# Two edge tiles per ScalarE sum in the first layer of a two-layer graph network: ranks packed into one number, split again on GpSimd, and a new written-out order

## The chip, the core and the metric

The kernel runs on one core of a Trainium2 chip. Time is device time in microseconds (us) of one execution. The engines are named as in the profile: PE (TensorE matmul) and PEld (its weight loads), DVE (VectorE), ACT (ScalarE), POOL (GpSimd) and SP (SyncE, which here only issues DMAs).

## The reference, cut to what matters

There are N = 12500 nodes with 256 features and E = 200000 edges `(src, dst, edge_weight)`, sorted by `dst`. The first layer computes, with `row = src` and `col = dst`:

```
feat_self, feat_nei = relu(x @ W[0] + b[0]), relu(x @ W[1] + b[1])     # 4 heads of 32
edge_w = (leaky(att_s)[row] + leaky(att_n)[col]) * adj_vals
agg    = segment_sum(edge_w * feat_nei[col], row)                      # sums over src
x      = layernorm(x + concat(norm(feat_self), norm(agg)))
```

The second layer sends `relu(x[src] @ W_a + x[dst] @ W_b + b)` to `dst`, sums it there, and ends in a linear update and two more normalisations. The change touches the first layer alone.

## The kernel before, in words

The edges come sorted by `dst`, while the first layer sums over `src`. So the first layer writes every edge's message into a log in DRAM, grouped by block of 128 source nodes (98 blocks and one for what is left over, `NBX` = 99; `NBE` = 100 is that made even). A second stage then reads the log block by block and sums. A third stage does the second layer.

**Groups.** The 1563 tiles of 128 edges are taken 14 at a time (`GT`), which makes 112 groups. `sort_tasks(g)` holds the tasks of a group as small functions, `feat_tasks(g)` those that compute node features, `meta_tasks` those that prepare edge data for eight groups at once. The tasks of one group, in the order of their data:

- `widen` (ACT, L564) copies the block numbers of the first 7 tiles into `bx`, each one 99 times. `hot` (DVE, L568) compares `bx` with a row of 0 to 98, which makes the one-hot rows `A` of those tiles. `hot_b` (DVE, L572) does the other 7 tiles straight from the block numbers, read with step 0. `pair` (DVE, L576) adds the halves into `B`.
- `ranks` (PE, L584), `quarter` (ACT, L587), `rows` (DVE, L591), `begins` (PE, L595 to L599) and `keep_begins`, `keep_v` (ACT, L603, L606) count the edges by block and give `v`: for each edge lane and block, the place where its run begins.
- `place_mm0` to `place_mm2` (PE, L622 and L624) write into a PSUM bank `wp`, for 5, 5 and 4 tiles, `v + BIG * A`, with `BIG` = 4096.
- `pick0` to `pick13` (ACT, L651) take one tile each: an ACTIVATE of `relu(w - BIG)` over 99 elements, whose sum (the one place of that edge) is written by a second instruction, the accumulator read, into a column of `sl`.
- `split` (DVE, L658 to L660), `hot_r`, `hot_q`, `goods` (DVE, L664, L674, L669: `rh`, `qh`, `mv`) and `permute` (PE, L681) turn places into a permutation by matmul; `mv` is the last DVE input of `permute`.
- `rel_keep` (ACT, L686: `rs`), `extras` (DVE, L697 copies the source row into the message tile `m`, L698 sums), `rel_turn`, `rel_row`, `rel_out`, `rel_in` (a row through DRAM and back, on SP's queue) and `hot_n` (DVE, L709: `oT`) make the one-hot matrices by target node.
- `message0` to `message5` (PE, L718) with `evict0` to `evict5` (ACT, L725) compute the messages into `m`, and `scatter0` to `scatter3` (POOL, L731) send `m` to the log by indirect DMAs.

**The order.** PE, ACT, DVE and SP run their instructions in the written order, and POOL runs its own in the order of the program. The dictionary `AT` gives each task a place; group `g`'s task is put at `256 * g + AT[name]`, and all tasks are issued in that order. So a group is spread over some seven periods of 256 steps, and within one period each engine works on tasks of several groups. An instruction whose input isn't ready holds everything behind it on its engine.

**Buffers.** PSUM has 8 banks: 2 for `wp`, 2 for the banks of the counts, 3 for `mp` (used by `permute` and the messages), 1 for `tp`.

Of the kernel before, what the change touches and what calls it, by code (L numbers as in the profile page):

```python
# [11 lines left out]
def _warn_once_fixed(msg, *args, **kwargs):  # L12
# [6 lines left out]
FT = mybir.dt.float32  # L19
FR = mybir.dt.float32r  # L20
BF = mybir.dt.bfloat16
I32 = mybir.dt.int32
AF = mybir.ActivationFunctionType
OP = mybir.AluOpType
AX = mybir.AxisListType

P = 128
# [3 lines left out]
GT = 14  # L31
NR = 16
RW = 4
MW = HD + H + 2
# [5 lines left out]
AT = {  # L40
    "widen": -453, "hot": -365, "hot_b": -265, "pair": -179, "ranks": -86, "quarter": -64, "rows": -29,
    "begins": 13, "keep_begins": 55, "keep_v": 51, "shift": 161, "reach": 262, "steps": 227, "steps_keep": 243,
    "steps_low": 256, "target": 313, "index": 400, "place_mm0": 52, "place_mm1": 63, "place_mm2": 204,
    "pick0": 73, "pick1": 78, "pick2": 78, "pick3": 87, "pick4": 123, "pick5": 144, "pick6": 156, "pick7": 170,
    "pick8": 179, "pick9": 219, "pick10": 229, "pick11": 239, "pick12": 249, "pick13": 280, "split": 339,
    "hot_r": 358, "goods": 374, "hot_q": 371, "permute": 424, "rel_keep": 435, "extras": 477, "rel_turn": 502,
    "rel_row": 552, "rel_out": 574, "rel_in": 595, "hot_n": 959, "message0": 997, "evict0": 1053,
    "message1": 1032, "evict1": 1063, "message2": 1056, "evict2": 1082, "message3": 1065, "evict3": 1121,
    "message4": 1101, "evict4": 1165, "message5": 1188, "evict5": 1203, "scatter0": 1120, "scatter1": 1146,
    "scatter2": 1197, "scatter3": 1206, "load": -331, "transposes": 47, "keep": 68, "project": 80, "relu": 295,  # L50
    "att_mult": 355, "mean_sum": 459, "att_sum": 438, "centre": 467, "leaky_n": 498, "part0": 584, "part1": 636,
    "part2": 665, "part3": 705, "leaky_s": 585, "out_f": 634, "m_load": -1689, "m_cast0": -1234,
    "m_cast1": -1433, "m_col0": -1201, "m_keep0": -1125, "m_col1": -698, "m_keep1": -614, "m_col2": -941,
    "m_keep2": -861, "m_block": -1073, "m_place": -877, "m_high": -378, "m_rest": -285, "m_mid": 263,
    "m_low": 351, "m_win": -76, "m_turn": -866, "m_pairs": -710, "m_mask": -535, "m_count": 210,
}
BIG = 4096.0
MAGIC = 1.5 * 2.0 ** 23
# [42 lines left out]
def kernel(  # L101
# [19 lines left out]
    nc = tc.nc  # L121
# [18 lines left out]
    NBX = NB + 1  # L140
    NBE = NBX + NBX % 2
# [74 lines left out]
    with ExitStack() as l0:  # L216
# [27 lines left out]
        nbig = dcp.tile([P, 1], FT, name="nbig")  # L244
        nc.vector.memset(nbig, -BIG)
        quart = dcp.tile([P, 1], FT, name="quart")
        capc = dcp.tile([P, 1], FT, name="capc")
# [59 lines left out]
        raw, blk, em, twin = {}, {}, {}, {}  # L307
# [240 lines left out]
        def sort_tasks(g):  # L548
# [4 lines left out]
            st = {}  # L553
            CH = [(0, 5), (5, 5), (10, 4)]

            def small(name, w=1, dt=FT, bufs=2, p=NBX):
                st[name] = srt.tile([p, w], dt, name=name, bufs=bufs)
                return st[name]
# [3 lines left out]
            def widen():  # L562
                st["bx"] = srt.tile([P, h, NBX], BF, name="bx")
                nc.scalar.copy(st["bx"], blk[c][:, j * GT:j * GT + h, None].to_broadcast([P, h, NBX]))  # L564

            def hot():
                st["A"] = srt.tile([P, GT, NBX], BF, name="A", bufs=3)
                nc.vector.tensor_tensor(st["A"][:, :h], iotab[:, :h], st["bx"], op=OP.is_equal)  # L568

            def hot_b():  # L570
                b = blk[c][:, j * GT + h:j * GT + GT, None].to_broadcast([P, h, NBX])
                nc.vector.tensor_tensor(st["A"][:, h:], iotab[:, h:], b, op=OP.is_equal)  # L572

# [31 lines left out]
            def keep_v():  # L605
                nc.scalar.copy(small("v", NBE, FR, p=P), st["V"])  # L606

# [9 lines left out]
            def place_mm(i):  # L617
                def f():
                    a, n = CH[i]
                    wp = st["w", i] = ps.tile([P, 512], FT, name="wp")  # L620
                    o = wp[:, :n * NBE].rearrange("p (t b) -> p t b", b=NBE)
                    nc.tensor.matmul(o, identr, st["v"][:, None, :].to_broadcast([P, n, NBE]),  # L622
                                     start=True, stop=False)
                    nc.tensor.matmul(o[:, :, :NBX], identk, st["A"][:, a:a + n],  # L624
                                     start=False, stop=True)
                return f
# [18 lines left out]

            def place_pick(t):
                def f():
                    i, k = divmod(t, 5)
                    if t == 0:
                        small("sl", GT, p=P)  # L650
                    nc.scalar.activation(small("junk", NBX, BF, p=P), st["w", i][:, k * NBE:k * NBE + NBX], AF.Relu,  # L651
                                         bias=nbig, accum_out=st["sl"][:, t:t + 1])
                return f

            def split():
# [39 lines left out]
            def extras():  # L695
                m = st["m"] = msgp.tile([P, NR, MW], FT, name="m")
                nc.vector.tensor_copy(m[:, :, MW - 2], st["go"][:, :, 1])  # L697
                nc.vector.tensor_reduce(m[:, :, MW - 1], st["go"][:, :, 2:5], AX.X, OP.add)  # L698

            def rel_out():  # L700
# [28 lines left out]
            def scatter(k):  # L729
                def f():  # L730
# [7 lines left out]
                    for p in zeros[-16:] if g >= GZ else zeros[:nz0] if g < 2 else []:  # L738
                        tc.add_manual_dep(ins, p.name, sync_dep, reason="the rows left over are zero")
                return f  # L740

            tasks = dict(widen=widen, hot=hot, hot_b=hot_b, pair=pair, ranks=ranks, quarter=quarter,
                         rows=rows, begins=begins, keep_begins=keep_begins, keep_v=keep_v, shift=shift, reach=reach,
                         steps=steps, steps_keep=steps_keep, steps_low=steps_low, target=target, index=index)
            tasks.update((f"place_mm{i}", place_mm(i)) for i in range(3))
            tasks.update((f"pick{t}", place_pick(t)) for t in range(GT))
            tasks.update(split=split, hot_r=hot_r, goods=goods, hot_q=hot_q, permute=permute, rel_keep=rel_keep,
                         extras=extras, rel_turn=rel_turn, rel_row=rel_row, rel_out=rel_out, rel_in=rel_in, hot_n=hot_n)
# [48 lines left out]

        work = defaultdict(list)
        for name, fs in (("hot_b", (first_nodes, lambda: load_group(1), load_norm_consts, bias_parts, bases)),
                         ("rows", (mt["m_high"], lead_zero, mt["m_rest"], mt["m_mid"], mt["m_win"])),  # L800
                         ("shift", (mt["m_turn"], mt["m_pairs"], mt["m_low"], consts_pairs)),
                         ("att_mult", (mt["m_mask"], mt["m_count"])),
                         ("centre", (consts_places, base_places))):
            work[min(AT[name], AT["split"] - 1) + 0.5] += fs

# [885 lines left out]
```

## Time and profile before

| | |
|---|---|
| five runs, median (lowest to highest) | 4010.7 us (4005.71 to 4014.55) |
| the profiled execution: time, span of its instructions | 4009.71 us, 4007.8 us |
| mean granted TensorE clock | 0.985 of full speed |
| first stage: first and last `hot_n` start | 50.7 us and 1059.5 us |
| second stage, the log's sums | about 1060 to 1990 us |
| third stage, the second layer | about 1990 us to the end |
| busy share of the whole span | PE 89%, PEld 74%, DVE 79%, ACT 59%, POOL 67% |

How to read it: busy shares are over the whole span; the stages have different limits, and the change lies in the first. In a timeline the columns are the start (us), the duration (us), the engine, the line, the operation and the tiles. ACT and DVE records overlap, since an instruction's start-up and drain run beside its neighbours. So what an instruction costs its engine is the time from its start to the next start, not its duration. A group row ends in busy time and the mean duration of one, then the idle time just before them.

### The profile page before, as it was taken

How to read it: one execution, taken by the hardware profiler on the slowest of the kernel's cores; microseconds unless marked ns; L12 is line 12 of the kernel's file. 1: busy time of each engine (PE TensorE's matmuls, PEld its weight loads, DVE VectorE, ACT ScalarE, POOL GpSimd, SP SyncE). 2: the span in 40 equal slices, each digit the busy share in tenths (PEclk: the TensorE clock that was granted, in tenths of full speed). 3: DMA queues.
4: the chain of work that ended last, by engine and by line, in shares of the span. 5: the costliest groups of instructions: out<-in, count | busy, mean ns of one | idle time of the engine just before them, and what ended most of it. 6: DMA issues, size and time to landing. Idle time of an engine off the chain costs nothing. (4 is left out here: it accounts for less than half of the span.)

```text
span 4007.8 us, 82564 instructions
## 1 busy us (share of the span) xinstructions
PE 3555.5 (89%) x24976; PEld 2971.5 (74%) x24976; DVE 3181.3 (79%) x9205; ACT 2377.1 (59%) x8379; POOL 2667.2 (67%) x2542
## 2 busy tenths in 40 slices
PE   8999999999899999999978888888888888888887
PEld 6888888887688888888866666666666666666665
DVE  8999999999799999999856666666666666666665
ACT  7999999999522222222255555555555555555555
POOL 2555555555666666666477777777777777777776
PEclk8999999999899999999999999999999999999999
DMA  5887866666666666666466666666666666666665
GB/s 176 277 275 272 275 219 220 218 216 200 219 185 193 184 195 192 187 192 194 145 182 171 170 172 170 170 169 171 173 169 171 171 171 170 170 172 172 170 171 135
DMA packets 470159, 763.55 MB, mean 191 GB/s; under 512 B 76202, under 2 KB 313504, under 8 KB 469712
## 3 DMA queue, kind: packets, MB, share of 16 engines
q1 hardware_dynamic: 339552, 415.13, 36.7%
q0 software_dynamic: 110848, 327.87, 27.2%
q10 hardware_dynamic: 19312, 15.21, 1.2%
q8 instruction: 204, 3.34, 0.3%
q14 instruction: 243, 1.99, 0.2%
HBM read 559.81 MB, written 198.12 MB: 189 GB/s over the span
## 5 line engine op out<-in xcount | busy, mean ns | idle before, releaser
L1346 POOL DMA_INDIRECT gb<-pd,srcf x1563 | 1508.4, 965 | 493.5 <-issue 237.1
L1405 DVE TENSOR_TENSOR gb<-qp,gb 128x512 f32<-128x512 f32 x781 | 538.7, 690 | 700.4 <-DMA gb<-pd,srcf 494.1
L1424 PE MATMUL agg<-gb,o 128*128 128x256 f32 x3126 | 857.5, 397 | 228.4 <-ACT gb L1407 224.3
L1407 ACT ACTIVATE gb<-gb 128x512 f32<-128x512 f32 x781 | 490.9, 629 | 846.9 <-DVE gb L1405 845.0
L731 POOL DMA_INDIRECT log<-m,ix x448 | 545.9, 1219 | 520.4 <-ACT m L725 149.5
L1424 PEld LDWEIGHTS agg<-gb,o 128*128 128x128 f32 x3126 | 562.3, 192 | 432.6 <-ACT gb L1407 371.3
L972 PE MATMUL sum<-lg,o 128*128 128x256 f32 x3724 | 838.4, 379 | 13.0 <-DMA lg<-log 12.0
L972 PEld LDWEIGHTS sum<-lg,o 128*128 128x128 f32 x3724 | 696.6, 189 | 112.0 <-POOL lg L959 12.2
L964 DVE TENSOR_SCALAR o<-iotap,lg 128x128 f32<-128x128 f32 x1862 | 612.7, 400 | 39.2 <-PE sum L972 29.8
L651 ACT ACTIVATE junk<-wp,nbig 128x99 bf16<-128x99 f32 x1568 | 606.6, 464 | 1.7 <-PE wp L624 1.4
L959 POOL TENSOR_TENSOR lg<-lg 128x512 f32<-128x512 f32 x392 | 429.3, 1107 | 226.6 <-DMA lg<-log 158.5
L1383 PE MATMUL qp<-qh,oT 128*128 128x256 f32 x1563 | 546.3, 372 | 1.0 <-DVE oT L1370 1.0
L651 ACT ACTIVATION_READ_ACCUMULATOR junk<-wp,nbig 128x1 f32 x1568 | 480.1, 320 | 0.0
L718 PE MATMUL mp<-F,oT 128*128 128x132 bf16 x5376 | 414.6, 222 | 14.2 <-DVE oT L709 3.4
L1383 PE MATMUL qp<-ql,oT 128*128 128x256 f32 x1563 | 407.9, 283 | 0.0
L718 PEld LDWEIGHTS <-oT 128*128 128x128 bf16 x5376 | 341.9, 98 | 44.1 <-DVE oT L709 13.1
L725 ACT COPY m<-mp 128x396 f32<-128x396 f32 (+1 forms) x672 | 353.2, 571 | 8.2 <-PE mp L718 7.9
L1383 PEld LDWEIGHTS qp<-qh,oT 128*128 128x128 f32 x1563 | 300.7, 192 | 19.4 <-DVE oT L1370 1.7
L1383 PEld LDWEIGHTS qp<-ql,oT 128*128 128x128 f32 x1563 | 301.0, 193 | 18.0
L1370 DVE TENSOR_SCALAR oT<-dr,baseP 128x256 fp32r<-128x256 int32 x782 | 293.4, 375 | 11.2 <-DMA dr<-in_dst_dram 11.1
L1391 ACT ACTIVATE o<-iotac,rel 128x128 f32<-128x128 f32 x782 | 265.5, 387 | 1.8 <-issue 1.6
L979 ACT COPY S<-sum 128x256 f32<-128x256 f32 x98 | 36.4, 372 | 292.0 <-PE sum L972 292.0
(263 smaller groups left out, 6421.8 us busy)
## 6 DMA issues: line engine op xcount, KB each, us to landing
lg<-log SPq DMA_DIRECT2D x392, 268.0 KB
dr<-in_dst_dram SPq DMA_DIRECT2D x781, 128.0 KB
rr<-reld SPq DMA_DIRECT2D x112, 512.0 KB
log<-zero SPq DMA_DIRECT2D x101, 268.0 KB
gb<-pd,srcf POOLq DMA_INDIRECT x1563
lg<-log SPq DMA_DIRECT2D x98, 201.0 KB
xw<-in_x_dram SPq DMA_DIRECT2D x112, 128.0 KB
xw<-x1d SPq DMA_DIRECT2D x112, 128.0 KB
```

What stands on the lines that cost most here:

```text
L651: nc.scalar.activation(small("junk", NBX, BF, p=P), st["w", i][:, k * NBE:k * NBE + NBX], AF.Relu, bias=nbig, accum_out=st["sl"][:, t:t + 1])
L718: nc.tensor.matmul(mp[:, r * (HD + H):(r + 1) * (HD + H)], st["oT"][:, r0 + r], F3[g][:, k], start=(k == 0), stop=(k == 2))
L725: nc.scalar.copy(st["m"][:, r0:r0 + n, 0:HD + H], st.pop(("mp", i))[:, :n * (HD + H)].rearrange("p (r w) -> p r w", r=n))
L731: ins = nc.gpsimd.indirect_dma_start(out=log[:, :], out_offset=bass.IndirectOffsetOnAxis(ap=st["ix"][:, k:k + 1], axis=0), in_=st["m"][:, ...
L959: e.tensor_tensor(t[:, 1, :n, 0:HD].rearrange("p r (h k) -> p r h k", h=H), t[:, 0, :n, 0:HD].rearrange("p r (h k) -> p r h k", h=H), t[:, ...
L964: nc.vector.tensor_scalar(o[:, r], iotap, t[:, 0, r, MW - 2:MW - 1], t[:, 0, r, MW - 1:MW], op0=OP.is_equal, op1=OP.mult)
L972: nc.tensor.matmul(sums[b], o[:, r], t[:, :, r, 0:HD], start=(k == 0 and r == 0), stop=(k == NK - 1 and r == n - 1))
L1346: nc.gpsimd.indirect_dma_start(out=gb[s][:r, i], out_offset=None, in_=pd[:, :], in_offset=bass.IndirectOffsetOnAxis(ap=srci[:r, t:t + 1], ...
L1383: nc.tensor.matmul(qp[:r, i], oT[:, i * P:i * P + r], q, start=(k == 0), stop=(k == 1))
L1405: nc.vector.tensor_tensor(z, qp, z, op=OP.add)
L1407: nc.scalar.activation(z, z, AF.Relu)
L1424: nc.tensor.matmul(agg[g], o[:r, i], z[:r, i], start=(j == 0 and i == 0), stop=lastmm)
```

## The change

- The `BIG` constant becomes 2^23, and `keep_w` (ACT) makes a second copy of the places, times `PACK` = 2048, beside `v`. The matmuls of `place_mm` now write `v` for even tiles and `2048 * v` for odd tiles. They take 4, 4, 4 and 2 tiles instead of 5, 5 and 4.
- A `pick` sums two tiles: 2 x 99 elements in one ACTIVATE and one accumulator read, 7 of each instead of 14. `unpack` (ACT, 7 elements per lane) divides by 2048, and `apart` (three POOL instructions, 7 elements per lane each) rounds and takes the two places apart into `sl`.
- `widen` copies all 14 tiles' block numbers, and `hot_b` reads that copy instead of the block numbers with step 0.
- The copy of the source row into `m` moves from DVE (`extras`) to ACT (`src_keep`).
- Nearly all places in `AT` are new. `permute`, for instance, moves from 424 to 536, `hot_n` from 959 to 1012, and the scatters from 1120 to 1206 to 1238 to 1272.

```diff
-BIG = 4096.0
+BIG = 2.0 ** 23
+PACK = 2048.0
...
+        nhalf = dcp.tile([P, 1], FT, name="nhalf")
+        nc.vector.memset(nhalf, 0.5 / PACK - 0.5)
...
-            CH = [(0, 5), (5, 5), (10, 4)]
+            CH = [(a, min(4, GT - a)) for a in range(0, GT, 4)]
...
             def widen():
-                st["bx"] = srt.tile([P, h, NBX], BF, name="bx")
-                nc.scalar.copy(st["bx"], blk[c][:, j * GT:j * GT + h, None].to_broadcast([P, h, NBX]))
+                st["bx"] = srt.tile([P, GT, NBX], BF, name="bx")
+                nc.scalar.copy(st["bx"], blk[c][:, tl, None].to_broadcast([P, GT, NBX]))
...
             def hot_b():
-                b = blk[c][:, j * GT + h:j * GT + GT, None].to_broadcast([P, h, NBX])
-                nc.vector.tensor_tensor(st["A"][:, h:], iotab[:, h:], b, op=OP.is_equal)
+                nc.vector.tensor_tensor(st["A"][:, h:], iotab[:, h:], st["bx"][:, h:], op=OP.is_equal)
...
             def keep_v():
-                nc.scalar.copy(small("v", NBE, FR, p=P), st["V"])
+                nc.scalar.copy(small("v", 2 * NBE, FR, p=P)[:, :NBE], st["V"])
+
+            def keep_w():
+                nc.scalar.activation(st["v"][:, NBE:], st["V"], AF.Copy, scale=PACK)
...
-                    nc.tensor.matmul(o, identr, st["v"][:, None, :].to_broadcast([P, n, NBE]),
+                    nc.tensor.matmul(wp[:, :n * NBE].rearrange("p (t b) -> p t b", b=2 * NBE), identr,
+                                     st["v"][:, None, :].to_broadcast([P, n // 2, 2 * NBE]),
                                      start=True, stop=False)
...
-            def place_pick(t):
+            def place_pick(k):
                 def f():
-                    i, k = divmod(t, 5)
-                    if t == 0:
-                        small("sl", GT, p=P)
-                    nc.scalar.activation(small("junk", NBX, BF, p=P), st["w", i][:, k * NBE:k * NBE + NBX], AF.Relu,
-                                         bias=nbig, accum_out=st["sl"][:, t:t + 1])
+                    i, t = k // 2, 2 * k % 4
+                    if k == 0:
+                        small("s7", h, p=P)
+                    nc.scalar.activation(
+                        small("junk", 2 * NBX, BF, p=P).rearrange("p (t b) -> p t b", b=NBX),
+                        st["w", i][:, t * NBE:(t + 2) * NBE].rearrange("p (t b) -> p t b", b=NBE)[:, :, :NBX],
+                        AF.Relu, bias=nbig, accum_out=st["s7"][:, k:k + 1])
                 return f
+
+            def unpack():
+                nc.scalar.activation(small("t7", h, p=P), st["s7"], AF.Identity, bias=nhalf, scale=1.0 / PACK)
+
+            def apart():
+                sl = small("sl", GT, p=P)
+                odd = sl.rearrange("p (k w) -> p k w", w=2)[:, :, 1]
+                nc.gpsimd.tensor_scalar(odd, st["t7"], MAGIC, -MAGIC, op0=OP.add, op1=OP.add)
+                even = sl.rearrange("p (k w) -> p k w", w=2)[:, :, 0]
+                nc.gpsimd.tensor_single_scalar(even, odd, PACK, op=OP.mult)
+                nc.gpsimd.tensor_tensor(even, st["s7"], even, op=OP.subtract)
...
             def extras():
                 m = st["m"] = msgp.tile([P, NR, MW], FT, name="m")
-                nc.vector.tensor_copy(m[:, :, MW - 2], st["go"][:, :, 1])
                 nc.vector.tensor_reduce(m[:, :, MW - 1], st["go"][:, :, 2:5], AX.X, OP.add)
+
+            def src_keep():
+                nc.scalar.copy(st["m"][:, :, MW - 2], st["go"][:, :, 1])
...
-    "widen": -453, "hot": -365, "hot_b": -265, "pair": -179, "ranks": -86, "quarter": -64, "rows": -29,
...
+    "widen": -426, "hot": -250, "hot_b": -221, "pair": -98, "ranks": 7, "quarter": 35, "rows": 57, "begins": 85,
...
+    "pick5": 298, "pick6": 298, "unpack": 326, "apart": 347, "split": 404, "hot_r": 420, "goods": 497,
+    "hot_q": 461, "permute": 536, "rel_keep": 572, "extras": 620, "src_keep": 622, "rel_turn": 600,
...
```

## The prediction

> **What bounds the kernel now.** The change lies in the first stage, so I first asked the table of busy time by stretch what that stage is limited by (columns: stretch, length, then busy us of PE, PEld, DVE, ACT, POOL, then clock and DMA).
>
> ```profile
> core 0: us, PE busy (x) PEld busy (x) DVE busy (x) ACT busy (x) POOL busy (x), PEclk, DMA share, GB/s
> 700.00:800.00 100.00, 97.92 (x1217) 83.50 (x1217) 98.32 (x312) 99.94 (x501) 55.51 (x45) 1.00 0.66 218
> ```
>
> ACT has no gap, DVE almost none, and PE is near; only POOL and the DMAs are free. The view of line L709 gives the length of the stage:
>
> ```profile
> L709 DVE TENSOR_SCALAR oT<-rr,pcol x112: 736/744/940, 50.7 to 1059.5; 128x2048 bf16<-128x2048 bf16 x112
> ```
>
> Its 17th to 97th starts lie 9.19 us apart on average; that is today's period per group, and 0.01 us on each of 112 periods is 1.1 us. ACT's timeline shows what a group costs there (start, duration):
>
> ```profile
> 501.45 0.50 ACT L651 ACTIVATE junk<-wp,nbig 128x99 bf16<-128x99 f32 x1
> 501.69 0.35 ACT L651 ACTIVATION_READ_ACCUMULATOR junk<-wp,nbig 128x1 f32 x1
> 501.78 0.49 ACT L651 ACTIVATE junk<-wp,nbig 128x99 bf16<-128x99 f32 x1
> ...
> 505.65 0.51 ACT L587 ACTIVATE rows<-fs,quart 99x1 f32<-99x1 f32 x1
> 505.80 0.60 ACT L651 ACTIVATE junk<-wp,nbig 128x99 bf16<-128x99 f32 x1
> ...
> 508.89 0.62 ACT L725 COPY m<-mp 128x396 f32<-128x396 f32 x1
> 509.27 0.91 ACT L564 COPY bx<-blk 128x693 bf16<-128x693 bf16 x1
> 509.94 0.73 ACT L466 COPY xT<-tp 128x512 f32<-128x512 f32 x1
> ```
>
> From start to next start, a pick costs 0.33 us (0.24 and 0.09), `widen` 0.67, an evict of 396 elements 0.38, one of 132 elements 0.15 (505.11 to 505.26). The two evicts give some 0.86 ns per element. DVE's timeline has the same for the two comparisons:
>
> ```profile
> 503.10 0.52 DVE L568 TENSOR_TENSOR A<-iotab,bx 128x693 bf16<-128x693 bf16 x1
> 503.53 0.51 DVE L365 SCALAR_TENSOR_TENSOR em<-mi,srcf 128x112 bf16<-128x112 int32 x1
> ...
> 506.58 0.87 DVE L572 TENSOR_TENSOR A<-iotab,blk 128x693 bf16<-128x693 bf16 x1
> 507.37 0.15 DVE L635 TENSOR_TENSOR dw<-fs,dh 99x1 bf16<-99x1 f32 x1
> ```
>
> **ACT, per period.** 14 picks at 0.326 (mean of the 80 periods) are 4.57 us. A pick over 198 elements costs 99 x 0.86 ns = 0.085 more, 0.41; seven are 2.88. Saved: 1.69. Added: 693 more elements of `widen`, 0.60 (to 0.67 if it simply doubles); `keep_w` 0.13, like `keep_v` (508.71 to 508.84), or 0.23 if it starts like a pick; `unpack` 0.15, like L587; `src_keep` 0.06, like `rel_keep` of the same shape (505.26 to 505.32). Sum: 9.19 - 1.69 + 0.94 = 8.44 us. ACT stops being the bound.
>
> **DVE, per period.** `hot_b` goes from 0.79 to 0.43, -0.36. The source-row copy L697 (506.25 to 506.34) leaves, -0.09. In the new order three instructions stand between `mean_sum` and `centre`, which waits for it; a reduction followed by its reader cost 0.44 (505.43 to 505.87), one that isn't 0.33 (504.23 to 504.56): -0.1. Sum: 8.64 us.
>
> **PE, per period.** PE's busy share is modelled, so I added the start-to-start times of its blocks of one line, each with the value of its quickest tenth of periods: 8.70 us, of which 0.13 is a wait of the first message for `oT`, and some 0.05 more is the edge data's transposes: 8.62. `place_mm`: two pairs of 500 columns at 0.31 + 0.23 and one of 400 at 0.27 + 0.18 are 1.53; three of 400 and one of 200 (0.18 + 0.09 by the same slope) are 1.62, +0.09. The messages run in four pieces instead of five or six, and a piece ahead of float32 work costs 0.62 instead of 0.535: about -0.06. Sum: 8.65 us.
>
> **POOL.** `apart` is new: three instructions over 7 elements per lane. No row shows such a one. The nearest on both sides:
>
> ```profile
> L1122 POOL TENSOR_TENSOR fs<-fs,scb 128x128 f32<-128x128 f32 x3 | 1.4, 457 | 13.5 <-ACT v L1007 13.2 <-ACT S L979 0.3
> L252 POOL IOTA roww<- 128x4 f32 x1 | 0.8, 819 | 0.0
> ```
>
> The same line at 384 elements is 997 ns, so 2.1 ns per element and 187 ns at none: 0.2 us each by this row (three, with 0.05 between, 0.7 us), 0.82 each by the iota. I take the first, as it is the same kind of arithmetic. POOL has the time: its four scatters are 4 x 1.22 us.
>
> What they cost DVE is the larger question. The second stage shows POOL and DVE at work together:
>
> ```profile
> 1451.46 1.42 DVE L989 TENSOR_TENSOR A<-A,S 128x512 f32<-128x512 f32 x1
> 1488.61 0.69 DVE L989 TENSOR_TENSOR A<-A,S 128x512 f32<-128x512 f32 x1
> ```
>
> ```profile
> 1451.22 1.11 POOL L959 TENSOR_TENSOR lg<-lg 128x512 f32<-128x512 f32 x1 [0.68 <-PE sum L972]
> ```
>
> Same instruction, twice the time: it started inside a POOL instruction that ended at 1452.33, and ended 0.55 later. So a DVE instruction with two SBUF inputs stands still until a POOL instruction that came first is done. With 0.2 us each, `apart` holds DVE between 0 and 0.6 us per period (a gain is excluded). In front of `split`, reductions and PSUM reads fill some 40% of DVE's time; an operation that is held loses 0 to 0.2, 0.1 on average. I take 3 x 0.1 x 0.6 = 0.2 us: DVE at 8.84.
>
> The Trainium skill speaks against the change here: "GPSIMD Engine Reference", section "When to use GPSIMD", puts elementwise work on VectorE, and "SBUF — State Buffer", section "SBUF: two separate sides", says the pair of ports is locked for a whole instruction, also against single-input DVE operations in a two-port mode, which no row here shows. By that rule I would take the full 0.6, and 9.24 us per period.
>
> **Waits that move.** A loop of one period runs through the new steps: `mv` (DVE) → `permute` → `rel_keep` → `unpack`, queued behind it on ACT → `apart` → `split` → the rest of DVE's group up to `mv`. Its length: `permute` 0.99, `rel_keep` 0.41, `unpack` 0.42, three hand-overs at 0.1, DVE from `split` to the end of `mv` 3.5 today (509.22 to 512.71) less 0.33 for `att_mult` plus about 0.95 for `pair`, `shift` and small ones moved in, 4.1: 6.2 us, and with 0.7 for `apart` 6.9. Under a period of 8.87 it has 1.9 us left; then DVE would wait at `split`, with `pair` and, behind it, PE's `ranks` late. POOL's queue puts `apart` behind `scatter3` of four groups earlier, which follows the last evict, 2.0 us of ACT's work ahead of `unpack`; a scatter of 1.2 fits, and of 1.8, as one at 510.48, too.
>
> SP's queue keeps its order (loads, `rel_out`, `rel_in`, `out_f`). `rel_in` to `hot_n` shrinks from 364 to 191 steps of the order, some 6.6 us; the broadcast row's packets are all in after 4.1 us (median; at most 5.8). Hidden, but with the scatters now in a burst the cover is thin; 1 us late would hold DVE 1 us.
>
> **Sum.** The longest engine is DVE at 8.84; today's 9.19 stands some 0.05 over the sum of DVE's and ACT's undisturbed intervals, of which I add 0.03. 8.87 us: 0.32 less on 112 groups, 35.8 us. The chain of one group, `widen` to `scatter3`, is 39 steps longer (1698 to 1659), 1.4 us once. Stages two and three are untouched. 4009.7 - 35.8 + 1.4 = 3975.3 for the profiled execution, which is 1.0 below the median: 3976.
>
> **The rivals.**
> - *The ports eat the gain.* Full price, 0.6: DVE at 9.24, between 9.1 and 9.24 per period, 4000 to 4016. For it: the L989 rows. Against: reductions, and the scatters, beside which L669 (1319 against 1320 ns) doesn't stretch. 0.13.
> - *Slower: the loop through POOL.* If each `apart` instruction takes the iota's 0.82, three with gaps and half a microsecond of waiting for DVE are 3.1, the loop 9.3 to 9.5, up to 0.3 over today: 4042. It decides from 2.65 us for `apart` on, and from 3.0 it is slower than before. Against: the 187 ns. 0.10.
> - *Better than summed.* The holds are nothing and PE's pieces pack better: 8.5 to 8.65 per period, 3930 to 3952. 0.05.
> - *The change doesn't do what it says.* A two-row operand costs ACT two picks' time: 9.19 + 0.94 = 10.1, 4115. Against: the three-row evicts keep their slope. 0.02.
> - The forecast, a period from 8.68 (no holds, PE's 8.65 sets it) to 9.08: 0.70.
>
> **How the numbers follow.** A measurement tells about 0.2% (8 us) from no change. Faster: 0.70 + 0.05 + 0.03 of the first rival = 0.78. Same: 0.08 of it. Slower: 0.02 of it + 0.10 + 0.02 = 0.14. The range runs from no holds with a little of the better case, 3951, up to 4010, inside the first rival; what lies beyond both ends is about 2 in 10.
>
> **What would show it.** Right: `hot_n` starts 8.7 to 9.0 us apart; ACT with some 0.4 us of gaps per period; a pair's pick at 0.41; POOL's new instructions near 0.2 us; DVE still over 97% busy, with some instructions ahead of `split` longer than before. Wrong: DVE idle in front of `split` with POOL as releaser (the loop); periods of 9.2 with DVE instructions stretched (the ports); `oT` waiting for `rr` (the burst).

## The result, and the profile after

The changed kernel takes 4011.1 us in the median of 26 runs (4003.9 to 4022.9), the kernel before 4010.1 us in the median of 47 (4003.1 to 4021.0): a ratio of 1.0005, 95% interval 1.0000 to 1.0011. Nothing was gained; 35 us were forecast. The profiled execution took 4007.4 us with a span of 4005.4 us.

The stretch shown of before (columns as there: stretch, length, busy us of PE, PEld, DVE, ACT, POOL, then clock, DMA share, GB/s), and the first stage from 100 to 1000 us as one stretch. First the kernel before:

```profile
core 0: us, PE busy (x) PEld busy (x) DVE busy (x) ACT busy (x) POOL busy (x), PEclk, DMA share, GB/s
100.00:1000.00 900.00, 867.92 (x10770) 738.10 (x10769) 883.44 (x2782) 897.18 (x4477) 483.36 (x393) 1.00 0.72 241
```

The changed kernel:

```profile
700.00:800.00 100.00, 96.05 (x1245) 86.17 (x1244) 94.53 (x304) 96.63 (x383) 69.45 (x77) 1.00 0.67 217
100.00:1000.00 900.00, 865.07 (x10933) 773.08 (x10932) 840.86 (x2682) 853.12 (x3381) 599.73 (x685) 0.98 0.72 240
```

Before, ACT was idle for 2.8 of 900 us and DVE for 16.6. After, ACT is idle for 46.9 and DVE for 59.1: the work did go, and no engine is full any more. Yet the last `hot_n` of the stage starts only 1.9 us sooner (1059.5 before), as the view of its line tells:

```profile
L730 DVE TENSOR_SCALAR oT<-rr,pcol x112: 740/747/858, 50.6 to 1057.6; 128x2048 bf16<-128x2048 bf16 x112
```

The mean of its 17th to 97th starts is 9.16 us (9.19 before), but the median is 8.83 (9.38 before), inside the forecast's 8.7 to 9.0: an undisturbed round of eight groups has periods of 8.8, 10.1, 8.2, 9.8, 8.8, 8.6, 9.5 and 8.4 (one of the kernel before: 9.4, 9.4, 9.4, 9.1, 8.5, 10.2, 8.6 and 8.6). So the question is what makes some periods long while three engines have gaps. The waits between 100 and 1000 us (engine, line, what it waited for: us in total, times, longest) name one, the second line here, that did not exist before:

```profile
POOL log L752 <- ACT m L746: 136.7, 99, 5.2
...
DVE sl L677 <- POOL sl L672: 30.6, 56, 1.2
...
PE mp L700 <- DVE mv L688: 17.8, 42, 0.5
```

It is `split` on DVE waiting for `apart` on POOL; the third is `permute` waiting for DVE, which is late for it. The first is POOL waiting for a message, of which there is plenty in both kernels and which costs nothing by itself.

The groups of instructions (line, engine, operation, tiles, count, then busy us, mean ns of one, idle time before and its releasers) have `apart` as three rows, 0.2 us each by the forecast:

```profile
L671 POOL TENSOR_SCALAR sl<-sl 128x7 f32<-128x7 f32 x112 | 48.9, 437 | 9.2
L669 POOL TENSOR_SCALAR sl<-t 128x7 f32<-128x7 f32 x112 | 47.6, 425 | 62.7 <-ACT t L664 60.0
L672 POOL TENSOR_TENSOR sl<-s,sl 128x7 f32<-128x7 f32 x112 | 25.2, 225 | 9.3
```

One period's walk, on POOL's timeline (start, duration, then the idle time and what ended it), where `unpack` ended on ACT at 720.98:

```profile
719.18 1.06 POOL L752 DMA_INDIRECT log<-m,ix  x1 [0.30 <-ACT F L517]
720.54 1.55 POOL L752 DMA_INDIRECT log<-m,ix  x1 [0.30 <-issue]
722.12 0.39 POOL L669 TENSOR_SCALAR sl<-t 128x7 f32<-128x7 f32 x1
722.59 0.75 POOL L671 TENSOR_SCALAR sl<-sl 128x7 f32<-128x7 f32 x1
723.42 0.20 POOL L672 TENSOR_TENSOR sl<-s,sl 128x7 f32<-128x7 f32 x1
```

On DVE's timeline the other end of it:

```profile
722.82 0.48 DVE L620 TENSOR_SCALAR Z<-iotaw,begun 99x512 bf16<-99x512 f32 x1
723.66 0.18 DVE L677 SCALAR_TENSOR_TENSOR sl<-sl,twin 128x14 f32<-128x14 f32 x1 [0.36 <-POOL sl L672]
...
726.92 1.32 DVE L688 TENSOR_TENSOR mv<-rh,em 128x1120 bf16<-128x1120 bf16 x1
```

`apart` was ready to run at 721.0 and stood behind a scatter until 722.12; its three instructions took 1.50 us; DVE had nothing to do for 0.36 us; and everything from `split` to `mv` moved by that. The widest of the three, L671, ended 0.04 us after L620, which DVE ran beside it.

The second thing is the clock. These are blocks of eight periods of the changed kernel, from one `hot_n` to the eighth after it (columns as above; the clock is the last number but two):

```profile
127.40:205.80 78.40, 75.38 (x899) 67.69 (x899) 69.20 (x220) 69.43 (x274) 46.23 (x56) 0.91 0.76 256
...
353.60:425.60 72.00, 69.62 (x901) 62.35 (x900) 68.69 (x220) 70.37 (x284) 47.56 (x57) 1.00 0.82 284
...
498.70:574.40 75.70, 73.79 (x899) 66.40 (x899) 69.16 (x220) 69.35 (x275) 47.86 (x57) 0.93 0.65 211
...
647.20:719.30 72.10, 69.84 (x901) 62.45 (x900) 68.49 (x219) 70.45 (x283) 50.21 (x57) 1.00 0.69 226
...
791.60:866.10 74.50, 71.07 (x899) 63.74 (x899) 68.91 (x219) 70.34 (x278) 51.65 (x57) 0.98 0.65 211
```

The same work takes 72.0 to 73.1 us where the clock stays at 1.00 (five blocks, mean 72.3), and up to 78.4 where it does not. In the records the clock falls to 0.5 nine times between 100 and 1000 us, for 3.4 or 6.8 us, 41 us in all. The kernel before has no such stretch there, and its blocks are more even (eleven of 73.3 to 74.4 us):

```profile
127.20:200.60 73.40, 71.16 (x882) 60.50 (x882) 72.11 (x227) 73.06 (x367) 39.03 (x33) 1.00 0.80 274
715.60:789.00 73.40, 71.49 (x888) 60.81 (x887) 72.16 (x228) 73.34 (x369) 39.38 (x33) 1.00 0.66 217
```

### The profile page after: what moved, and what is told of

Read it like the earlier page. It is cut to its first block, busy times and chain, and to the rows that moved or that the text cites. A ratio compares the mean times of both kernels' runs of the same rounds, so it can differ in the third digit from the quotient of the medians.

```text
span 4005.4 us, 82506 instructions
## 1 busy us (share of the span) xinstructions
PE 3552.3 (89%) x25200; PEld 3010.7 (75%) x25200; DVE 3126.3 (78%) x9094; ACT 2331.1 (58%) x7147; POOL 2802.2 (70%) x2878
## 5 line engine op out<-in xcount | busy, mean ns | idle before, releaser
L752 POOL DMA_INDIRECT log<-m,ix x448 | 561.1, 1252 | 301.9 <-ACT m L746 152.1
L739 PE MATMUL mp<-F,oT 128*128 128x132 bf16 x5376 | 392.6, 223 | 2.1 <-ACT F L521 1.3
L657 ACT ACTIVATE junk<-wp,nbig 128x198 bf16<-128x198 f32 x784 | 337.4, 466 | 1.5 <-PE wp L630 0.9
L746 ACT COPY m<-mp 128x396 f32<-128x396 f32 (+1 forms) x672 | 292.1, 470 | 14.2 <-PE mp L739 10.7
L1415 ACT ACTIVATE o<-o,ones 128x256 f32<-128x256 f32 x391 | 198.8, 508 | 12.7
```

What stands on the lines that cost most here:

```text
L657: nc.scalar.activation(small("junk", 2 * NBX, BF, p=P).rearrange("p (t b) -> p t b", b=NBX), st["w", i][:, t * NBE:(t + 2) * NBE].rearrang ...
L739: nc.tensor.matmul(mp[:, r * (HD + H):(r + 1) * (HD + H)], st["oT"][:, r0 + r], F3[g][:, k], start=(k == 0), stop=(k == 2))
L746: nc.scalar.copy(st["m"][:, r0:r0 + n, 0:HD + H], st.pop(("mp", i))[:, :n * (HD + H)].rearrange("p (r w) -> p r w", r=n))
L752: ins = nc.gpsimd.indirect_dma_start(out=log[:, :], out_offset=bass.IndirectOffsetOnAxis(ap=st["ix"][:, k:k + 1], axis=0), in_=st["m"][:, ...
```

## The experiments

Two theories. **The loop:** mv, permute, rel_keep, unpack, apart, split and back to mv has no slack, because it takes longer than the 6.9 us of the prediction; it makes a block without half clock (a clean block) 72.3 us instead of 71.0 (8 x 8.87). **The clock:** stretches at half clock, which come with PE's waits for DVE, take back what is left. The rival that the ports hold DVE is answered by the trace (below). The runs come in groups, each with the kernel before beside it; in some groups the chip ran the third stage longer, and the kernel before takes 4379 to 4410 us instead of 4009, so a ratio is to be read against its own group. The changed kernel itself ran in two of the groups only, in `b1_changed` and `d0_changed`; where a run of another group is held against `b1_changed`, that is said. Three variants ran both in the group of `b1_changed` and in the first one (names with e), and there their ratios are 0.14 to 0.39% higher.

### The control, apart on DVE, and two scatters moved (kernel before beside them: 4008.9 us)

`d0_changed` is the changed kernel itself, `d3_before_here` the kernel before, profiled.

> The changed kernel itself, as the control for this call. Both theories: about 1.01 of the kernel before where the kernel before takes 4380 to 4410 us, 1.0005 where it takes 4010.

> The kernel before, profiled on the same chip. If the place costs stage 3 alone: hot_n starts again 9.19 us apart and ends by 1060 us, and the whole difference to 4010 us is in stage 3. If the first stage is slowed for every kernel, its period is 9.5 or more here, and the ratios of the experiments are too kind to nobody: they stand against an equally slowed stage.

Measured: 4007.5 us, ratio 1.0001 (0.9992 to 1.0010); and for the kernel before `hot_n` 9.22 us apart from 50.4 to 1058.4 us, without a stretch at half clock. In this group the kernel before takes its first time again, so what the first stage of the kernel before does in the other groups was not seen; the question of `d3_before_here` stays open but for a difference: there, 4407 less 4009 is 398 us, of which the third stage makes some 395 (2414 against 2019 us by the traces of the changed kernels), so its first two stages hardly lose. The control repeats the picture: five of twelve blocks without half clock, mean 72.35 us; among the others 73.4 to 75.4, the last and shorter one apart.

`d1_apart_dve` takes the sums apart ahead of `split` on DVE:

```
-  nc.gpsimd.tensor_scalar(odd, st["t7"], MAGIC, -MAGIC, op0=OP.add, op1=OP.add)
-  nc.gpsimd.tensor_single_scalar(even, odd, PACK, op=OP.mult)
-  nc.gpsimd.tensor_tensor(even, st["s7"], even, op=OP.subtract)
...
+  nc.vector.tensor_scalar(sl[:, :, 1], st["t7"], MAGIC, -MAGIC, op0=OP.add, op1=OP.add)
+  nc.vector.scalar_tensor_tensor(sl[:, :, 0], sl[:, :, 1], -PACK, st["s7"], op0=OP.mult, op1=OP.add)
...
   "apart": 347 -> 403
```

> The sums are taken apart by two instructions on DVE, directly ahead of split, instead of three on POOL; the result is the same. Loop theory: the loop is shorter by POOL's 1.0 to 1.9 us and by the wait behind scatters (0.3 to 1.2), and longer by 0.35 on DVE; the wait at split goes, DVE's own sum is 8.4 + 0.35 = 8.75, and the mean period falls from 9.16 to about 8.9 (or by as much from 9.5): 20 to 40 us less than the control. Theory of three full engines: any instruction that goes onto DVE lengthens the period, and the hand-overs between PE, ACT and DVE cost as before: 0 to 40 us more than the control.

Measured: 4006.8 us, 0.9997 (0.9986 to 1.0007): no change. On its DVE timeline:

```profile
719.91 0.20 DVE L668 TENSOR_SCALAR sl<-t 128x7 f32<-128x7 f32 x1
720.14 0.17 DVE L669 SCALAR_TENSOR_TENSOR sl<-sl,s 128x7 f32<-128x7 f32 x1
720.35 0.18 DVE L674 SCALAR_TENSOR_TENSOR sl<-sl,twin 128x14 f32<-128x14 f32 x1
```

The two cost 0.44 us from start to start here and 0.40 in the mean (0.35 was expected), since each waits for the one before. The wait at `split` is gone from the list, as the loop theory had it, but DVE pays 0.40 us of work for a wait that was 0.3 us per period (30.6 us over some 98 periods), and is nearly full where nothing disturbs it:

```profile
300.00:400.00 100.00, 96.26 (x1242) 85.95 (x1239) 97.73 (x323) 97.05 (x383) 55.02 (x45) 1.00 0.81 279
```

Its clean blocks take 72.7 us. So the 20 to 40 us of the loop theory did not come: the loop through POOL costs as much as the same work on DVE does, and the half clock stays (44 us in 96 periods).

`d2_scatter_late`: `"scatter2": 1268 -> 1375, "scatter3": 1272 -> 1379`, behind `apart` in POOL's order.

> scatter2 and scatter3 of a group are issued on POOL behind apart of the group that follows, not ahead of it. If what costs in the loop is POOL's queue (a scatter of 1.05 to 1.6 us that apart stands behind, 37 us of the chain in stage 1), the time falls by 15 to 40 us below the control. If it is apart's own instructions, nothing changes, and a message tile that comes free later costs up to 10 us.

Measured: 4008.3 us, 0.9997 (0.9986 to 1.0008). The edit did not reach what it aimed at: POOL still issues four scatters between one `apart` and the next, and the other two now come late instead. `apart` starts 0.56 us after `unpack` in the mean (0.59 and 0.61 in the two traces of the changed kernel). It says nothing against the queue as a cause; an `apart` that really stands ahead of the scatters was not tried.

### apart done twice

```
+  for _ in range(2):
     (the three instructions on POOL)
```

> apart's three instructions are done twice. Loop theory: the loop grows by another 1.0 to 1.4 us in each period and has no slack, so the time rises by 0.6 to 1.2 us x 112 = 65 to 130 us over the changed kernel. Port theory: the price is what DVE loses beside POOL, 0 to 0.6 us more per period with DVE's own instructions longer: 0 to 65 us, and no more wait at split. If apart has slack, nothing changes.

Measured: 4507.2 us, 1.0219 (1.0205 to 1.0232); the kernel before beside it 4409.6. The changed kernel did not run in this group. It reached 1.0098 (1.0076 to 1.0120) in the group of `b1_changed` (below); against that the second `apart` costs 1.2%, 53 us or 0.47 us per period, and, as an estimate, 0.8 to 1.1% if this group lies as much higher as the three variants that ran in both. The three added instructions are 0.95 us long (0.37, 0.36 and 0.22). At most half of it reaches the period, less than the 65 to 130 us of the loop theory, and the wait at `split` grows:

```profile
DVE sl L678 <- POOL sl L673: 95.9, 77, 2.0
```

95.9 us in 77 waits, against 37.5 in 60 for `b1_changed`. So a longer `apart` does lengthen the wait and the time: it is on the path that sets the period in part of the groups. But this run also has 136 us at half clock between 100 and 1000 us (22 stretches), where `b1_changed` has 72 (16), so part of the price is the clock's, and the run does not divide the two.

### apart left out

ACT copies the two halves instead of POOL's three instructions; the sums are not taken apart.

```
+  nc.scalar.copy(sl[:, :, 1], st["t7"])
+  nc.scalar.copy(sl[:, :, 0], st["s7"])
...
   "apart": 347 -> 327
```

> The changed kernel itself, as the control of the runs beside it, since the first four were made where the kernel before takes 4407 us and not 4010. If the place is like that of the first measurement: 4005 to 4018 us, ratio 1.000 to 1.002, about nine half-clock stretches between 100 and 1000 us. If it is the slow one again: 4440 to 4480 us, ratio 1.008 to 1.016 as the four variants there.

> The changed kernel without the three POOL instructions: unpack's value and the packed sum are copied into sl by two small ACT copies behind unpack, so split reads places that are not taken apart (that part of the computation is left out). Theory A: POOL's 1.0 to 1.9 us and its queue leave the loop, two ACT copies of about 0.15 us each come in; the period falls to 8.65 to 8.85 us, 3955 to 3980 us. Theory B: only what the waits of PE lose in the half-clock stretches, 3995 to 4012 us. Theory C: 4005 to 4015 us.

> Without the three POOL instructions (places not taken apart, two small ACT copies in their stead), to be held against the changed kernel run beside it. Theory A: 25 to 50 us under it. Theories B and C: within 12 us of it.

Measured: the control `b1_changed` 4424.1 us, 1.0098 (1.0076 to 1.0120); without `apart` 4406.6 us, 1.0060 (1.0037 to 1.0082) beside it, and 1.0079 (1.0061 to 1.0097) in the group of the next three experiments, where no control ran. It is some 17 us better than the control, with intervals that overlap a little, and less than the 25 to 50 us of the loop theory. The sign is the loop's, and it is some 0.15 us per period with the two copies on ACT in the place of POOL. But here too the half clock moved with it, from 72 us to 37, so the 17 us are not the loop's alone.

The control also shows that the changed kernel suffers there and the kernel before hardly does. Its `hot_n`:

```profile
L730 DVE TENSOR_SCALAR oT<-rr,pcol x112: 735/745/760, 48.6 to 1102.1; 128x2048 bf16<-128x2048 bf16 x112
```

45 us later than in the first profile, with 72 us at half clock and further waits of ACT's `quarter` for PE (20 us in two rows of the list). The operations keep their durations. Why its waits grow there stays open.

### unpack earlier, and the loop opened

`e1_unpack_early` and `b2_unpack_early`: `"unpack": 326 -> 300`, ahead of `rel_keep` on ACT.

> The changed kernel with one number changed: unpack stands at 300 in the order, ahead of rel_keep (316 in the same steps), no longer behind it at 326. Theory A (the loop mv, permute, rel_keep, unpack, apart, split, mv sets the period): the loop is cut, since unpack no longer stands behind an instruction that waits for permute; DVE's waits for POOL at split go below 0.05 us per period, the period falls from 9.18 to 8.65 to 8.80 us, the time to 3955 to 3975 us. Theory B (PE's half-clock stretches alone cost the gain, and they come from PE's wait for mv, which stays): the stretches stay, 4000 to 4012 us. Theory C (DVE's uneven work for the edge data sets it): no change, 4005 to 4015 us.

> unpack at 300 instead of 326, ahead of rel_keep, to be held against the changed kernel run beside it. Theory A (the loop over permute, rel_keep, unpack and POOL sets the period): 30 to 50 us under the changed kernel. Theory B (half-clock stretches of PE): within 10 us of it, unless the waits for mv go too. Theory C (uneven work for the edge data on DVE): within 10 us of it.

Measured: 4469.7 us, 1.0123 (1.0104 to 1.0143), and 4421.0 us, 1.0109 (1.0082 to 1.0136); the control is 1.0098. No gain. By the order of the queues `unpack` then waits for the last pick, that for the last `place_mm`, and that stands behind `ranks` on PE, which waits for `pair` on DVE: another loop of one period. `c1_free` takes this one away too:

```
   "place_mm3": 265 -> 251, "pick4": 292 -> 270, "pick5": 298 -> 272, "pick6": 298 -> 274
   "unpack": 326 -> 276, "apart": 347 -> 290
```

> The last placing block, its picks, unpack and apart are moved ahead of ranks and of permute, so that nothing they need comes out of the same period's ranks or permute. Loop theory: with the loop opened, DVE's wait at split for POOL's last instruction (0.36 us per period on average) goes, and the period falls from the changed kernel's 9.16 (9.5 at the slower place) by 0.2 to 0.36 us: 22 to 40 us off the changed kernel. Clock theory: the stretches at half clock come from the wait of ranks and permute for DVE and stay; the loop's end only moves the wait, and the time changes by less than 10 us. Rival: ranks now stands behind one more block on PE (0.27 us) and quarter behind three picks on ACT; if the second loop split, hot_r, pair, ranks, steps is the tight one, the time rises by up to 30 us.

> The same opened loop, and ten small bfloat16 matmuls in front of permute, where PE waits. Loop and clock theory together: the half-clock stretches of stage 1 shrink to fewer than 4, worth about 10 us, beside what the opened loop gives. If the loop is not what costs, this run is 10 us from the changed kernel, and no better than the filler alone.

Measured: 4599.6 us, 1.0439 (1.0425 to 1.0454), and with the filler 4525.3 us, 1.0268 (1.0253 to 1.0283): the rival won, by five times its price (some 150 us, with `b1_changed`'s ratio as the control). DVE's timeline of `c1_free`, and below it ACT's:

```profile
705.67 0.42 DVE L489 TENSOR_TENSOR tm<-R,atb 128x256 f32<-128x256 f32 x1
707.99 0.15 DVE L593 TENSOR_SCALAR rows<-rows 99x1 f32<-99x1 f32 x1 [1.90 <-ACT junk L657]
```

```profile
706.96 0.43 ACT L657 ACTIVATE junk<-wp,nbig 128x198 bf16<-128x198 f32 x1
707.27 0.21 ACT L657 ACTIVATION_READ_ACCUMULATOR junk<-wp,nbig 128x1 f32 x1
707.51 0.30 ACT L664 ACTIVATE t<-s,nhalf 128x7 f32<-128x7 f32 x1
707.72 0.24 ACT L589 ACTIVATE rows<-fs,quart 99x1 f32<-99x1 f32 x1
```

`quarter` (L589) now stands behind three picks and `unpack`, and DVE waits 1.9 us for it; PE's `project` waits for it too. The wait at `split` is no longer among DVE's longer ones, and the period is 10.9 us. In this kernel an earlier place in one queue is a later one for somebody else, and more than one loop through DVE is close to the period.

`c2_free_fill` differs from `c1_free` in the ten filler matmuls alone and ran in the same group. The first stage of both, `c1_free` first:

```profile
100.00:1000.00 900.00, 788.75 (x9289) 692.62 (x9287) 715.77 (x2255) 753.39 (x2860) 510.11 (x577) 0.92 0.61 208
100.00:1000.00 900.00, 827.58 (x10717) 730.35 (x10715) 755.95 (x2389) 799.37 (x3032) 552.35 (x612) 0.99 0.63 219
```

The half clock between 100 and 1000 us falls from 143 us (29 stretches) to 24 (5), and the time falls by 74 us, the filler's own work included. That is 0.6 us for each us at half clock, and of all runs this pair shows best that the clock has a price.

### Filler matmuls ahead of permute

```
+  for _ in range(10):    # five in f2_fill5
+      nc.tensor.matmul(bank_p[:, P:2 * P], identb, identb, start=True, stop=True)
```

> The changed kernel with ten bf16 matmuls of 128 columns, whose result nobody reads, ahead of permute in the same PSUM bank (about 0.55 us of PE work per period at the place where PE waits 0.65 us for mv). Theory A: the loop is as long as before, the time stays within 10 us of 4011. Theory B: the nine half-clock stretches between 100 and 1000 us go, and with them 0.15 us per period or 17 us: 3990 to 3998 us.

> Ten bf16 matmuls of 128 columns that nobody reads ahead of permute, to be held against the changed kernel run beside it. Theory B: the half-clock stretches go and 13 to 21 us with them. Theory A: within 10 us, the loop being as long.

> Ten bfloat16 matmuls ahead of permute, in a column range that nothing reads. Clock theory: the stretches at half clock go (11 in stage 1 of the control, 41 to 51 us in sum, each costing half its length), blocks of eight periods all take about 72.3 us, and the time falls by 15 to 22 us below the kernel before: 3987 to 3995. Loop theory alone: the stretches go and the time stays, because the matmuls only fill a wait for DVE; 4005 to 4012. Rival: the ten cost PE 0.55 us in periods where it has no gap, and the time rises by up to 20 us.

> Five of them: 0.3 us in a gap of 0.65 to 0.75. Clock theory: if that is enough to keep the clock, the same gain or a few us more than with ten; if not, stretches remain and the time lies between the control (4007) and the run with ten.

Measured, in this order: 1.0115 (1.0100 to 1.0130); 1.0076 (1.0059 to 1.0093); 1.0082 (1.0068 to 1.0096); with five 1.0065 (1.0051 to 1.0078). The control `b1_changed`, in the group of the second alone, is 1.0098. The half clock falls from its 16 stretches (72 us between 100 and 1000 us) to 6, 3 and 2 (24, 14 and 8 us) with ten matmuls, and to 8 (42 us) with five. Against that control the last three gain 7 to 15 us with intervals that touch, and the first, in a group without a control, gains nothing. The gain may be as small as that because the filler costs too: with ten, the blocks without half clock take 75.3 us (11 blocks), where the control's two such take 73.6 and 74.5. None of these ran where the kernel before takes 4009 us, so there the clock's price rests on the blocks, not on a run without the stretches, and the 3987 to 3995 us that were expected of ten matmuls were not put to the test.

`c3_no_apart_fill` joins both edits:

> POOL's three instructions are replaced by two small copies on ACT (the split of the sums is left out, so the places are wrong numbers) and the ten filler matmuls are there. If the loop's length through POOL and the clock each cost on their own, the gains add: 17 us (apart) and 10 us (filler) below the changed kernel. If both are one cause (DVE late, so PE late, so half clock), the sum is no more than 17.

Measured: 4484.7 us, 1.0171 (1.0157 to 1.0185), worse than either alone (1.0060 to 1.0115). Its stretches at half clock are few (6, 31 us), and in five windows of 100 us no engine is over 96% busy. The sum that was expected did not come, and why is open.

### The changed work in the old order

`e4_old_order` keeps the kernel before's order and puts the new steps into it.

> The changed kernel's work in the order of the kernel before: the old places for all tasks that both have, pick k where pick 2k+1 was, place_mm3 at 215, keep_w with keep_v at 51, unpack 290, apart 300, src_keep 478. There unpack does not stand behind a rel_keep that waits for the same period's permute, but split follows at 339. Theory A: no loop over POOL as long as a period; the lighter ACT and DVE show, 3965 to 3990 us. Theory C (the new order is needed for the gain): 4010 us or more.

Measured: 4479.7 us, 1.0164 (1.0151 to 1.0177). It has no stretch at half clock, its periods are regular, and 9.9 us long, with one wait in nearly every group:

```profile
DVE sl L758 <- POOL sl L753: 75.8, 91, 1.2
```

So of the two orders the new one is the better for the changed work (9.2 us, and 9.5 in `b1_changed`); and half clock does not come with the changed work as such, but with where it stands.

## Why the prediction was wrong, point by point

**The engines' sums were right.** ACT: 8.44 us forecast, 8.55 by the undisturbed start-to-start times after. A pair's pick, from start to start 0.40 (0.41 forecast); `hot_b` 0.43 as forecast; `widen` 1.24, by 0.57 more, not 0.60. DVE: 8.64 forecast without holds, 8.60 found. Here they are on ACT's timeline:

```profile
720.49 0.30 ACT L705 CAST rs<-mp 128x16 bf16<-128x16 f32 x1
720.60 0.38 ACT L664 ACTIVATE t<-s,nhalf 128x7 f32<-128x7 f32 x1
720.81 1.41 ACT L567 COPY bx<-blk 128x1386 bf16<-128x1386 bf16 x1
...
724.74 0.43 ACT L657 ACTIVATE junk<-wp,nbig 128x198 bf16<-128x198 f32 x1
725.06 0.20 ACT L657 ACTIVATION_READ_ACCUMULATOR junk<-wp,nbig 128x1 f32 x1
725.15 0.43 ACT L657 ACTIVATE junk<-wp,nbig 128x198 bf16<-128x198 f32 x1
```

**The port's 0.2 us did not fall on DVE.** The same DVE instructions last as long beside `apart` as without it: L489 400 against 408 ns, L519 287 and 287, L620 483 and 481, L503 406 and 405. It is POOL's that are longer. L671 takes 0.26 us in the 18 groups where DVE is idle beside it, and 0.75 in the median of the 36 where DVE runs L503 and then L620; in all of those it ends 0.04 us after L620 does. That fits a POOL instruction that stands still until DVE's are done, but no run tested it. By the Trainium skill, "SBUF — State Buffer", section "SBUF: two separate sides", the one that starts first keeps the shared pair of ports for its whole instruction, and the other waits. Here L503 starts before L671 and L620 after it, so the order of starts alone does not give the wait that the trace shows. The prediction priced the case in which DVE waits; in this trace it is POOL's instructions that grow, and what POOL loses lies in the loop.

**The failed step is the loop's length, "6.9 us" with "1.9 us left".** Means over 90 periods of the changed kernel:

| term | forecast | measured |
|---|---|---|
| permute | 0.99 | 0.99 |
| rel_keep, unpack and hand-overs | 1.13 | 1.20 |
| `apart` waiting in POOL's queue | within a hand-over | 0.58 (up to 1.66) |
| `apart` | 0.7 | 1.28 (0.9 to 1.9) |
| `split` to the end of `mv` | 4.1 | 4.58 (4.0 to 6.5) |
| sum | 6.9 | 8.63 |

The rest to 9.20 is slack before `split`, and it is not there when it is needed: in 53 of the 90 periods DVE starts `split` within 0.1 us of POOL's end. Each of the three terms was costed by its quietest case: an instruction of seven elements by POOL alone (it stretches to 1.05 us while DVE works), a scatter that "fits", and DVE's part without the edge data's pieces (up to 1.1 us in a period; periods without them and without a wait do take 4.1). A mean slack does not serve periods that differ by 1.9 us, as these do in an undisturbed round; the kernel before is uneven too (8.5 to 10.2). The chain of waits says the same: of some 900 us followed back from the last `hot_n` that ended before 1000 us, the kernel before spends 482 on DVE and 252 on ACT; the changed one 302 on DVE, 265 on ACT, 147 on PE and 62 on POOL.

**What was not foreseen at all is the clock.** The prediction gave PE's waits no price beyond their own length; its sum has no term for it, and the changed kernel spends 41 of 900 us at half clock.

**Where the 35 us went.** The profiled execution is 32 us over its forecast (4007.4 against 3975.3). Clean blocks give 9.04 us per period instead of the forecast 8.87: 0.17 x 112 = 19 us. In these blocks DVE is idle for 0.45 us per period, and 0.30 of that is `split` waiting for POOL: the loop. So 8.60 of work and 0.45 of idle time make the 9.04, where the forecast had 8.64, 0.2 of holds and 0.03. What is left to the mean of 9.16, 0.12 us, would be 13 us. The eleven full blocks from 127 to 938 us take 810.9 us, where eleven clean ones would take 11 x 72.34 = 795.7: 15 us lost in the blocks with half clock. That the stretches cost this is an agreement of blocks, in two traces of the changed kernel; `c1_free` and `c2_free_fill` show that the clock has a price, in another order of the tasks. Part of it may be the waits that come with the stretches, since in the six disturbed blocks DVE is idle for 0.73 us per period. So the two causes are read from the traces; no run here takes one away and leaves the other as it was, and how the 32 us divide between them is an estimate.

**The rivals.** The loop through POOL (0.10) was the right mechanism, at the wrong point: it was said to decide from 2.65 us for `apart` on, and did from about half of that, as queue and DVE's part had used up the slack. The ports' rival gave a range that the time falls into, 4000 to 4016, but by luck: it had DVE's instructions stretched, and the trace shows POOL's. Loads and `rel_in` stayed hidden: `hot_n` waited for `rr` twice, 2.0 us in all.

## What to carry to other kernels

When the fullest engine is relieved, the next bound can be a loop through several queues, sooner than the next engine's sum. Cost each of its terms by the loaded case, queue waits included, and compare it with the longest period, not the mean, before a step on a fourth engine is put into it. Taking some 5% of the busy time off two engines was worth nothing here, where waits came in its place; look at whether TensorE's granted clock is still 1.00 in every stretch.

## What the runs showed of the hardware

- **Half clock after short waits.** The nine stretches of the changed kernel are 3.41 or 6.83 us long, and all nine start on one grid of 3.413 us, to within 0.001 us; so do the stretches in each of the other traces that have any. In the 3.5 us before each, PE is idle twice, for 0.1 to 0.9 us ahead of `ranks` and 0.4 to 0.5 ahead of `permute`, 0.6 to 1.4 us in sum. The Trainium skill, "TensorE: Matmul & The Clock Gate", section "What's actually happening", has the half rate and the window of 3413 ns, and these lengths and the grid agree. Its section "Why this matters for your kernels" asks for no idle gaps over some 3 us; here none is over 0.9, so by this measurement that is not enough. But of the 19 windows of the grid at full clock in which PE is idle for 0.6 us or more, only 8 were followed by half clock, and in the kernel before none of 13 to 17 such windows (by where the grid is laid) was. What tips it is open.
- **POOL's small instructions beside DVE.** Seven elements per lane: 0.20 to 0.38 us for the two-operand form, 0.25 to 1.05 us for the one with a scalar; 0.20 and 0.26 with DVE idle beside them. DVE's instructions kept their length.
- **The new sum over two rows.** 198 elements in one ACT instruction with its accumulator read cost 0.40 us where two of 99 cost 0.65.
